# The last seven steps of a two-layer graph kernel: source order, an accumulating last gather, a second store queue

## The chip, the cores and the metric

The kernel runs on one core of one Trainium2 chip. The metric is device time in microseconds (us) of one execution. The core has a matrix engine (TensorE, PE in the profile), a vector engine (VectorE, DVE), an activation engine (ScalarE, ACT), GpSimd (POOL) and a queue engine (SyncE, SP). Each has its own instruction stream; they meet through semaphores. SP, ACT and POOL issue DMAs.

## The reference, cut to what matters

Two layers over a graph of N = 3327 nodes with 512 features and a dense 3327 x 3327 adjacency, all in float32:

```python
# layer 0: attention with the adjacency as bias
h = jnp.maximum(_layernorm(x, axis=-1), 0.0)
a = q @ k.T * scale + adj + adj                 # q, k, v: h times Wq, Wk, Wv
x = x + jax.nn.softmax(a, axis=-1) @ v
# layer 1: normalized adjacency, applied twice
h = jnp.maximum(_layernorm(x, axis=-1), 0.0)
A2 = adj + jnp.eye(N)
dscale = jnp.diagonal(A2) ** (-0.5)
temp = A2 @ h @ W.T
x = x + jax.nn.relu((dscale[:, None] * A2 * dscale[None, :]) @ temp)
```

## The kernel before

N is padded to 3328 = 26 tiles of 128 rows. After the scores, three large products remain: attention weights times h (g = 0), A2 times h (g = 1) and A2 times the scaled temp (g = 2). Each is done by a fast matrix product on two levels. On the outer level both operands are cut in halves, and seven products `p5, p1, p6, p7, p2, p3, p4` (in this order) of sums of quarters give the four quarters of the result. Each outer product has 13 x 13 tiles and is computed in two column strips, s = 0 (7 tiles wide per half) and s = 1 (6 wide). Within a strip the inner level does the same again: six pairs of tiles, t = 0 to 5, each of seven matmuls (L762) into seven PSUM banks also called p1 to p7, and a last, odd tile (t = None) with four plain matmuls (L754) into p2, p3, p4 and an eighth bank, p8 (bank 3). A matmul shows as two records in the profile.

So there are 3 x 7 x 2 x 7 steps, and `run(k)` (L963) does for step k, in this order: loads the left operand of step k+3 (`left`, L669, on SP; if the tile meets the diagonal, a 128x128 VectorE add of the identity, L686, comes with it); the matmuls; on an odd step, the gather; on VectorE the sums of step k+2 (L171 to L173, which make four sums of the loaded quarters in one of three `o` slots); what the gather left for later; and what is attached to the step in `between`. Loads go round five `a` slots.

The gather (L765) turns the eight banks into the product's four quarters: ScalarE copies p1 (L796), and VectorE does eight adds from PSUM (L797 to L806). The function `settle` then adds the product into the outer result in SBUF, whose quarters are r11 to r22; p4 goes into r21, two adds of full width (L792). For p4 of strip 1 that is split by columns into `lo` and `hi`: `settle(lo)` stands between the sixth and the seventh bank add, `settle(hi)` behind the next sums.

When rows of a result are ready, a job on them is attached to a step. For g = 0 and 1 it is a product with weights (L838, bank 3) and what follows; for g = 2 it is `finish` (L876): PE transposes the columns of a tile (L884) into a bank `pt`, ScalarE applies relu and the scale (L886), VectorE adds the loaded row `xr` (L887), and GpSimd stores it (`store`, L87). While steps still run, `pt` is bank 3; its load, `finish_load` (L871), is issued on ACT one step earlier, into a ring of four. Tiles 17, 7 and 18, 8 and 9 and 19, 10, 11 and 12, and 13 belong to steps 0 to 5 of the last strip. Of tiles 20 to 25 the right half of the features is finished earlier (in p2 to p4); the left half (256 columns) waits for the last gather and uses the six other banks.

The order of instructions on each engine is fixed in two ways. Inside the context `in_order` (L120) every engine keeps the source's order. Outside it the framework's scheduler orders each engine's instructions by its own estimate. Before, the first part ends at the last product's second strip (`last`, L982): its seven steps and the final finishes are the scheduler's.

At the very end `tc.If` (L1365) branches on a flag `bad`, computed early in group 0, to a general kernel that isn't needed here. `values_load` reads the flag into a register of each engine.

Of the kernel before, what the change touches and what calls it, by code (L numbers as in the profile page):

```python
# [15 lines left out]
P = 128  # L16
# [28 lines left out]
def graph_layers_kernel(  # L45
# [28 lines left out]
    nc = tc.nc  # L74
    N = out.shape[0]
    NP, D = x.shape
    DC = D // P
    NT = NP // P
    scale = 1.0 / math.sqrt(D)
    E = D // 2  # L80

    def pieces(n):

        m = n - n % 16
        return [(0, m), (m, n)] if m and m < n else [(0, n)]

    def store(dst, src, n):  # L87
        for a, z in pieces(n):
            nc.gpsimd.dma_start(dst[a:z], src[a:z])  # L89

# [15 lines left out]
    def bank(k, name):  # L106
        return banks.tile([P, BW], F32, name=name, tag=f"bank{k}")

    def ring(*slots):

        turn = itertools.cycle(slots)

        def take(shape, name):
            kind, k = next(turn)
            return kind(k, shape, name)

        return take
# [47 lines left out]
    x1d = [dram.tile([P, D], F32, name=f"x1d{i}") for i in range(NT)]  # L165
# [62 lines left out]
    class Chain:  # L228
# [60 lines left out]
    ps = [bank(k, "mm") for k in range(DC)]  # L289
# [116 lines left out]
    class Pair:  # L406
# [97 lines left out]
    steps = [(n, t) for n in range(len(groups)) for t in range(HALF)]  # L504
# [32 lines left out]
    with in_order(*(e.engine for e in (nc.vector, nc.tensor, nc.gpsimd, nc.sync))):  # L537
# [9 lines left out]
        k = len(steps)  # L547
# [18 lines left out]
    def seven():  # L566
        return {r: bank(ROLE[r], r) for r in ("p1", "p6", "p7", "p5", "p2", "p3", "p4")}
# [82 lines left out]
    cts = {}  # L650

    def set_up():

        free = [view(k, j)[:, 2 * m : 2 * m + 2] for k, j in ((2, 2), (3, 0), (3, 1), (3, 2)) for m in range(2)]
        free = [f.rearrange("p a w -> p (a w)") for f in free] + [mid(k, [P, H[0]], f"ct{k}") for k in range(10)]
        for s in range(2):
            cts[s] = [[free.pop()[:, : H[s]] for d in range(DC)] for y in range(2)]
        cts["to"] = [free.pop() for k in range(2)]
# [4 lines left out]
    ts_ring = ring(*spare[:3])  # L663
    xr_ring = ring(*spare[:3], (half, 14))
    out_ring = ring((half, 12), (half, 13), *spare[3:])
    xr_last = ring(*((half, k) for k in (4, 5, 6, 7)), (mid, 10), (mid, 11))
    out_last = ring((half, 12), (half, 13), *spare[2:], (half, 14))

    def left(g, s, what, t):  # L669
# [19 lines left out]
    class Right:  # L689
# [9 lines left out]
        def rows(self, dst, h, z):  # L699

            for k, i in enumerate(self.its):
                src = rowd[self.g][h * HALF + i]
                nc.sync.dma_start(dst[:, k], src if z is None else src[:, z * E : (z + 1) * E])
# [58 lines left out]
                nc.tensor.matmul(ps[r][:, :w], b[:, i], m, start=self.t == 0,  # L762
                                 stop=self.t == PAIRS - 1 and r in ("p1", "p5", "p6", "p7"))

    def gather(ct, r, s, ps):  # L765

        hw, qw = H[s], Q[s]

        def region(y, z):
            return [ct[y][2 * z + k] for k in range(2)]  # L770

        place = {"p5": (1, 1), "p1": (0, 0)}.get(r)
        if place:
            to = region(*place)
        else:
            to = [cts["to"][k][:, :hw] for k in range(2)]
        p = {k: v[:, :qw] for k, v in ps.items()}
        lo, hi = slice(0, qw), slice(qw, hw)
        r11, r12, r21, r22 = region(0, 0), region(0, 1), region(1, 0), region(1, 1)

        def settle(w):

            for k in range(2):
                if r == "p6":
                    nc.vector.tensor_sub(r12[k][:, w], to[k][:, w], r11[k][:, w])
                elif r == "p7":
                    nc.vector.tensor_add(r21[k][:, w], to[k][:, w], r12[k][:, w])  # L787
                    nc.vector.tensor_sub(r12[k][:, w], r22[k][:, w], r12[k][:, w])  # L788
                    nc.vector.tensor_sub(r22[k][:, w], r21[k][:, w], r22[k][:, w])  # L789
                elif not place:  # L790
                    into = {"p2": r11, "p3": r12, "p4": r21}[r]
                    nc.vector.tensor_add(into[k][:, w], into[k][:, w], to[k][:, w])  # L792


        c11, c12, c21, c22 = to[0][:, lo], to[1][:, lo], to[0][:, hi], to[1][:, hi]
        nc.scalar.copy(c11, p["p1"])  # L796
        nc.vector.tensor_sub(c22, p["p6"], c11)  # L797
        nc.vector.tensor_add(c21, c22, p["p7"])
        nc.vector.tensor_sub(c12, c22, p["p5"])
        nc.vector.tensor_sub(c22, c21, p["p5"])  # L800
        nc.vector.tensor_add(c11, c11, p["p2"])
        nc.vector.tensor_sub(c12, p["p3"], c12)
        if r == "p4" and s == 1:
            settle(lo)
        nc.vector.tensor_add(c21, c21, p["p4"])
        nc.vector.tensor_add(c22, c22, p["p8"])  # L806
        return lambda: settle(hi if r == "p4" and s == 1 else slice(0, hw))

    def where(i):

        s = int(i >= STRIPS[1])
        return (s, *divmod(i - STRIPS[s], HT[s]))
# [55 lines left out]

    xrs = {}

    def finish_load(i, z=(0, 1), spot=None):  # L871
        c0, c1 = z[0] * E, (z[-1] + 1) * E
        xrs[i] = (xr_ring if spot is None else xr_last)([P, D], "xr")
        nc.scalar.dma_start(xrs[i][:, c0:c1], x1d[i][:, c0:c1])

    def finish(i, z=(0, 1), spot=None):  # L876

        s, y, k = where(i)
        n = min(P, N - i * P)
        c0, c1 = z[0] * E, (z[-1] + 1) * E  # L880
        xr = xrs[i]
        pt = bank(ROLE["p8"] if spot is None else spot, "pt")
        for d in range(c0 // P, c1 // P):
            nc.tensor.transpose(pt[:, d * P : (d + 1) * P], cts[s][y][d][:, k * P : (k + 1) * P], ident)  # L884
        o = (out_ring if spot is None else out_last)([P, D], "r")
        nc.scalar.activation(o[:, c0:c1], pt[:, c0:c1], AF.Relu, scale=sd[:, i : i + 1])  # L886
        nc.vector.tensor_add(o[:, c0:c1], o[:, c0:c1], xr[:, c0:c1])  # L887
        store(out[i * P : i * P + n, c0:c1], o[:n, c0:c1], n)

    every = (*range(PAIRS), None)  # L890
    rights = {(g, r, t): Right(g, r, t) for g in range(3) for r in ORDER for t in every}
    steps = [Step(g, r, s, t, rights[g, r, t]) for g in range(3) for r in ORDER for s in range(2) for t in every]
# [3 lines left out]
    def number_of(g, r, s, t):  # L896
        return ((g * len(ORDER) + r) * 2 + s) * len(every) + t
# [5 lines left out]
    for g in range(3):  # L903
        for n, r in enumerate(ORDER):
            for t, e in enumerate(every):
                k = number_of(g, n, 0, t)
# [11 lines left out]
    for n, job in enumerate(jobs):  # L918
        k = k0 + n * (k1 - k0) // len(jobs)
# [3 lines left out]
    def rows(g, k, i, *z):  # L923

        if g == 0:
            at(k - 1, attend_load, i)
            at(k, attend, i)
            at(k + 1, attended, i)
        elif g == 1:
            at(k, temp, i)  # L930
        else:
            at(k - 1, finish_load, i, *z)
            at(k, finish, i, *z)
# [12 lines left out]
                rows(g, number_of(g + 1, 0, 0, 0) + 2 * k, i)  # L946
    for t, i in enumerate((17, 18, 19)):
        rows(2, number_of(2, 6, 1, t), i)
    for t, i in enumerate(range(20, NT)):
        rows(2, number_of(2, 4, 0, t), i, (1,))  # L950
    for k, what in ((1, totals), (2, prepare), (6, prepared), (8, judge), (9, judged)):
# [9 lines left out]
    banks_of = {}  # L961

    def run(k):  # L963
        step = steps[k]
        if k + 3 < len(steps):
            steps[k + 3].load()
        if step.t == 0:
            banks_of.update(seven())
        if not cts:
            set_up()  # L970
        if step.t is None:
            banks_of["p8"] = bank(ROLE["p8"], "p8")
        step.multiply(banks_of)
        rest = gather(cts[step.s], step.r, step.s, banks_of) if step.t is None else None
        if k + 2 < len(steps):
            steps[k + 2].sums()
        if rest:
            rest()
        for what, args in between.get(k, ()):
            what(*args)  # L980

    last = number_of(2, 6, 1, 0)  # L982
    with in_order(*(e.engine for e in (nc.vector, nc.tensor, nc.gpsimd, nc.scalar, nc.sync))):
        for k in range(last):
            run(k)
    for k in range(last, len(steps)):
        run(k)
    for i in range(20, NT):
        finish_load(i, (0,), True)
    for n, i in enumerate(range(20, NT)):  # L990
        finish(i, (0,), (0, 2, 4, 6, 7, 1)[n])


@with_exitstack
def general_kernel(
# [373 lines left out]
```

## Time and profile before

| | |
|---|---|
| median of 4 runs | 2242.48 us (2237.17 to 2244.7) |
| the profiled execution | 2238.98 us |
| its span, first to last instruction | 2236.8 us |
| granted TensorE clock, mean | 0.994 |
| PE busy | 2181.8 us |
| VectorE busy | 1623.4 us |
| ScalarE busy | 230.8 us |
| last L887 add, end | 2222.63 us |
| last store of GpSimd, start | 2224.4 us |
| matmuls of L754 of the last step, start | 2215.28 us |

Times within the profile count from the start of the span. A line of the timeline is: start, length, engine, source line, operation, tiles written and read, shape, count of like instructions merged, and in brackets how long the engine had been idle before it and what ended that. In the chain of waits each line is: start, length, what the end was waiting for in that stretch. A stretch of merged instructions lasts from the first's start to the last's end, and records of one engine overlap by some hundredths of a microsecond, so what an instruction costs is read from the distance between starts.

### The profile page before, as it was taken

What the parts mean: (1) busy time and instruction counts of PE and PEld (TensorE: products, weight loads), DVE (VectorE), ACT (ScalarE), POOL (GpSimd) and SP (SyncE); (2) the same over time, 40 slices, a digit from 0 to 9 for tenths busy, and PEclk for the clock granted to TensorE, in tenths of its full rate; (3) what the DMA queues carried; (4) which work ended last, traced back from release to release, by engine and by line L of the source; (5) the groups of instructions that cost most, each with busy time, mean ns of one, the idle gap of its engine ahead of it and who ended that gap; (6) DMA issues with size and microseconds to landing.
All of it is one profiled execution on the core that took longest, in us unless ns stands there. A gap on an engine that the chain in (4) does not pass through costs nothing. (4 is left out here: it accounts for less than half of the span.)

```text
span 2236.8 us, 20973 instructions
## 1 busy us (share of the span) xinstructions
PE 2181.8 (98%) x6252; PEld 1162.9 (52%) x6252; DVE 1623.4 (73%) x3095; ACT 230.8 (10%) x336; POOL 357.0 (16%) x555
## 2 busy tenths in 40 slices
PE   8999999999999999999999999999999999999996
PEld 4555555455555555555444555555554555555554
DVE  6369888788877788877777778886543458777775
ACT  4422121112110000000010000000000000000011
POOL 4223333333321000001222110000000000000001
PEclk9999999999999999999999999999999999999998
DMA  6668888888969898887787899876636458765684
GB/s 242 209 209 302 295 296 285 303 283 308 356 203 334 322 367 282 281 300 270 259 297 241 300 340 344 288 276 201 220 120 202 145 170 296 243 200 185 210 302 153
DMA packets 246412, 583.68 MB, mean 261 GB/s; under 512 B 34770, under 2 KB 105904, under 8 KB 246288
## 3 DMA queue, kind: packets, MB, share of 16 engines
q1 hardware_dynamic: 191968, 399.15, 53.9%
q0 software_dynamic: 45104, 167.88, 19.8%
q10 hardware_dynamic: 9216, 15.21, 2.2%
q8 instruction: 52, 0.85, 0.2%
q14 instruction: 72, 0.59, 0.1%
HBM read 414.28 MB, written 167.85 MB: 260 GB/s over the span
## 5 line engine op out<-in xcount | busy, mean ns | idle before, releaser
L762 PE MATMUL p<-part,b 128*128 128x448 f32 (+1 forms) x3528 | 1256.2, 514 | 6.9 <-DVE part L172 4.9
L762 PEld LDWEIGHTS p<-part,b 128*128 128x128 f32 x3528 | 668.2, 190 | 575.2 <-issue 301.0
L171 DVE TENSOR_TENSOR part<-part 128x896 f32<-128x896 f32 (+1 forms) x252 | 256.9, 1019 | 85.8 <-PE p L762 38.4
L439 PE MATMUL Y<-qt,hp 128*128 128x448 f32 (+1 forms) x832 | 308.9, 514 | 4.2 <-DVE g L443 3.1
L439 PEld LDWEIGHTS Y<-qt,hp 128*128 128x128 f32 x832 | 157.2, 190 | 139.8 <-issue 73.0
L439 PE MATMUL Z<-qt,hp 128*128 128x384 f32 (+1 forms) x416 | 162.6, 513 | 0.0
L173 DVE TENSOR_TENSOR part<-part,part 128x448 f32<-128x448 f32 (+1 forms) x219 | 129.5, 591 | 17.5 <-PE p L762 0.9
L172 DVE TENSOR_TENSOR part<-part,part 128x448 f32<-128x448 f32 (+1 forms) x219 | 129.4, 591 | 7.3
L838 PE MATMUL p<-w,ct 128*128 128x512 f32 x272 | 125.5, 601 | 5.3 <-DVE part L850 3.6
L754 PE MATMUL p<-part,b 128*128 128x448 f32 (+1 forms) x336 | 124.2, 513 | 0.0
L439 PEld LDWEIGHTS Z<-qt,hp 128*128 128x128 f32 x416 | 78.8, 190 | 67.4 <-issue 36.2
L443 DVE SCALAR_TENSOR_TENSOR g<-g,Y 128x384 f32<-128x384 f32 (+1 forms) x156 | 91.4, 586 | 27.1 <-PE Y L439 24.6
L832 POOL DMA_DIRECT2D sum<-job x52 | 28.4, 547 | 488.2 <-DVE job L829 269.1
L797 DVE TENSOR_TENSOR part<-p,part 128x384 f32<-128x384 f32 (+1 forms) x33 | 19.3, 586 | 104.3 <-ACT part L796 57.1
L754 PEld LDWEIGHTS p<-part,b 128*128 128x128 f32 x336 | 63.5, 190 | 53.7 <-issue 32.6
L838 PEld LDWEIGHTS p<-w,ct 128*128 128x128 f32 x272 | 51.8, 192 | 67.3 <-issue 52.0
L796 ACT COPY part<-p 128x384 f32<-128x384 f32 (+1 forms) x33 | 16.5, 499 | 669.1 <-PE p L762 669.1
L439 PE MATMUL X<-qt,hp 128*128 128x384 f32 (+1 forms) x208 | 81.1, 512 | 0.0
L446 ACT ACTIVATE g<-g 128x768 f32<-128x768 f32 (+1 forms) x48 | 43.0, 896 | 352.4 <-DVE g L443 296.5
L838 PE MATMUL p<-w,part 128*128 128x512 f32 x144 | 67.6, 607 | 5.2 <-DVE ct L806 5.2
L431 POOL DMA_DIRECT2D sum<-o x52 | 36.8, 708 | 220.1 <-DVE o L425 155.6
L89 POOL DMA_DIRECT2D out_dram<-r x34 | 18.4, 542 | 305.0 <-DVE r L887 276.5
(157 smaller groups left out, 1868.8 us busy)
## 6 DMA issues: line engine op xcount, KB each, us to landing
part<-sum SPq DMA_DIRECT2D x104, 448.0 KB, 5.2
part<-p SPq DMA_DIRECT2D x91, 448.0 KB, 6.3
part<-sum SPq DMA_DIRECT2D x104, 384.0 KB, 3.5
part<-p SPq DMA_DIRECT2D x91, 384.0 KB, 4.2
part<-in_adjT_dram SPq DMA_DIRECT2D x78, 448.0 KB, 4.9
b<-row SPq DMA_DIRECT2D x234, 128.0 KB, 4.9
part<-in_adjT_dram SPq DMA_DIRECT2D x78, 384.0 KB, 3.7
g<-in_adjT_dram SPq DMA_DIRECT2D x52, 448.0 KB, 4.5
```

Source lines behind the costliest of these rows:

```text
L171: nc.vector.tensor_add(o[:, 0:2], g[:, 0:4:3], g[:, 1:2].to_broadcast([P, 2, g.shape[-1]]))
L172: nc.vector.tensor_add(o[:, 2], o[:, 1], g[:, 0])
L173: nc.vector.tensor_add(o[:, 3], o[:, 2], g[:, 2])
L431: nc.gpsimd.dma_start(self.to(sumd)[:, 0:2], self.o)
L439: nc.tensor.matmul(ps[:, :wd], h_of(self.t, name, k), qt[B[name]][:, k], start=start and k == 0, stop=k == 1, skip_group_check=True)
L443: nc.vector.scalar_tensor_tensor(a[n], a[n], 2.0, ps[:, :wd], op0=ALU.mult, op1=ALU.add if sign > 0 else ALU.subtract)
L446: nc.scalar.activation(g[1], g[1], AF.Exp, **({"bias": pad} if self.t == HALF - 1 else {}))
L754: nc.tensor.matmul(ps[("p2", "p3", "p4", "p8")[k]][:, :w], b[:, z], a[:, 0, y], start=k == 3, stop=True)
L762: nc.tensor.matmul(ps[r][:, :w], b[:, i], m, start=self.t == 0, stop=self.t == PAIRS - 1 and r in ("p1", "p5", "p6", "p7"))
L797: nc.vector.tensor_sub(c22, p["p6"], c11)
L832: nc.gpsimd.dma_start(sumd[self.s][self.j][:, 2 + self.k], self.a)
L838: nc.tensor.matmul(ps, cts[s][y][d][:, k * P : (k + 1) * P], w[d], start=d == 0, stop=d == DC - 1)
```

## The change

Four edits. First, the last gather of all (p4, strip 1, g = 2) adds straight into r21: the first four bank adds are made into a scratch tile as before, four adds bring them into the four pieces of r21, and four more add the banks p2, p3, p4 and p8 directly. In the two earlier groups the gather of p4, strip 1, is now like all others: eight bank adds, the sums, and then one settle of full width. Second, `in_order` now spans all steps and the final finishes; the loads of the left halves of tiles 20 to 25 are attached to steps 2, 3 and 4 of the last strip, two at a time, into three tiles. Third, the last finishes store by GpSimd and SP in turn (the tile of 127 rows, number 25, has two pieces, both on SP). Fourth, the flag is read within the last gather, after the four adds into r21, on every engine.

```diff
-    def store(dst, src, n):
+    def store(dst, src, n, queue=nc.gpsimd):
         for a, z in pieces(n):
-            nc.gpsimd.dma_start(dst[a:z], src[a:z])
+            queue.dma_start(dst[a:z], src[a:z])
...
-    xr_last = ring(*((half, k) for k in (4, 5, 6, 7)), (mid, 10), (mid, 11))
+    xr_last = ring(*((half, k) for k in (4, 5, 6)))
...
-        def settle(w):
-
-            for k in range(2):
-                if r == "p6":
-                    nc.vector.tensor_sub(r12[k][:, w], to[k][:, w], r11[k][:, w])
...
+        into = r21 if last else None
...
-        nc.vector.tensor_add(c11, c11, p["p2"])
-        nc.vector.tensor_sub(c12, p["p3"], c12)
-        if r == "p4" and s == 1:
-            settle(lo)
-        nc.vector.tensor_add(c21, c21, p["p4"])
-        nc.vector.tensor_add(c22, c22, p["p8"])
-        return lambda: settle(hi if r == "p4" and s == 1 else slice(0, hw))
+        if into is None:
+            nc.vector.tensor_add(c11, c11, p["p2"])
+            nc.vector.tensor_sub(c12, p["p3"], c12)
+            nc.vector.tensor_add(c21, c21, p["p4"])
+            nc.vector.tensor_add(c22, c22, p["p8"])
+        else:
+
+            o11, o12, o21, o22 = (t[k][:, w] for t, k, w in ((into, 0, lo), (into, 1, lo), (into, 0, hi), (into, 1, hi)))
+            nc.vector.tensor_add(o11, o11, c11)
+            nc.vector.tensor_sub(o12, o12, c12)
+            nc.vector.tensor_add(o21, o21, c21)
+            nc.vector.tensor_add(o22, o22, c22)
+            flags.append(nc.values_load(bad, min_val=0, max_val=1))
+            for o, k in ((o11, "p2"), (o12, "p3"), (o21, "p4"), (o22, "p8")):
+                nc.vector.tensor_add(o, o, p[k])
+
+        def settle():
+            for k in range(2):
...
+                elif not place and into is None:
+                    t = {"p2": r11, "p3": r12, "p4": r21}[r]
+                    nc.vector.tensor_add(t[k], t[k], to[k])
...
+    def last_load(i):
+
+        xr = xr_last([P, 2, E], "xr")
+        for k in range(2):
+            xrs[i + k] = xr[:, k]
+            nc.scalar.dma_start(xr[:, k], x1d[i + k][:, 0:E])
...
+    for n, i in enumerate(range(20, NT, 2)):
+        at(number_of(2, 6, 1, 2) + n, last_load, i)
...
-    last = number_of(2, 6, 1, 0)
     with in_order(*(e.engine for e in (nc.vector, nc.tensor, nc.gpsimd, nc.scalar, nc.sync))):
-        for k in range(last):
+        for k in range(len(steps)):
             run(k)
-    for k in range(last, len(steps)):
-        run(k)
-    for i in range(20, NT):
-        finish_load(i, (0,), True)
-    for n, i in enumerate(range(20, NT)):
-        finish(i, (0,), (0, 2, 4, 6, 7, 1)[n])
-
+        for n, i in enumerate(range(20, NT)):
+            finish(i, (0,), (0, 2, 4, 6, 7, 1)[n], (nc.gpsimd, nc.sync)[n % 2])
+    return flags[0]
...
-            graph_layers_kernel(tc, x_in, *rest, out, bad)
-            with tc.If(nc.values_load(bad, min_val=0, max_val=1) > 0):
+            with tc.If(graph_layers_kernel(tc, x_in, *rest, out, bad) > 0):
                 general_kernel(tc, x_in[: x.shape[0]], adj_in, *rest, out)
```

More of the change, by code (lines that the diff above doesn't have):

```diff
@@ L763, in multiply, with gather @@
                                  stop=self.t == PAIRS - 1 and r in ("p1", "p5", "p6", "p7"))
-    def gather(ct, r, s, ps):
+    flags = []
+    def gather(ct, r, s, ps, last):
         hw, qw = H[s], Q[s]
@@ L779, in gather @@
         r11, r12, r21, r22 = region(0, 0), region(0, 1), region(1, 0), region(1, 1)
-        def settle(w):
-            for k in range(2):
-                if r == "p6":
-                    nc.vector.tensor_sub(r12[k][:, w], to[k][:, w], r11[k][:, w])
[L786 to L792, printed above, removed]
+        into = r21 if last else None
         c11, c12, c21, c22 = to[0][:, lo], to[1][:, lo], to[0][:, hi], to[1][:, hi]
@@ L800, in gather @@
         nc.vector.tensor_sub(c22, c21, p["p5"])
-        nc.vector.tensor_add(c11, c11, p["p2"])
-        nc.vector.tensor_sub(c12, p["p3"], c12)
-        if r == "p4" and s == 1:
-            settle(lo)
-        nc.vector.tensor_add(c21, c21, p["p4"])
-        nc.vector.tensor_add(c22, c22, p["p8"])
-        return lambda: settle(hi if r == "p4" and s == 1 else slice(0, hw))
+        if into is None:
[14 more added lines that the diff above has]
+            for k in range(2):
+                if r == "p6":
+                    nc.vector.tensor_sub(r12[k], to[k], r11[k])
+                elif r == "p7":
+                    nc.vector.tensor_add(r21[k], to[k], r12[k])
+                    nc.vector.tensor_sub(r12[k], r22[k], r12[k])
+                    nc.vector.tensor_sub(r22[k], r21[k], r22[k])
+                elif not place and into is None:
+                    t = {"p2": r11, "p3": r12, "p4": r21}[r]
+                    nc.vector.tensor_add(t[k], t[k], to[k])
+        return settle
     def where(i):
@@ L869, in graph_layers_kernel, with finish_load, finish @@
     xrs = {}
-    def finish_load(i, z=(0, 1), spot=None):
+    def finish_load(i, z=(0, 1)):
         c0, c1 = z[0] * E, (z[-1] + 1) * E
-        xrs[i] = (xr_ring if spot is None else xr_last)([P, D], "xr")
+        xrs[i] = xr_ring([P, D], "xr")
         nc.scalar.dma_start(xrs[i][:, c0:c1], x1d[i][:, c0:c1])
-    def finish(i, z=(0, 1), spot=None):
+    def last_load(i):
[3 more added lines that the diff above has]
+            nc.scalar.dma_start(xr[:, k], x1d[i + k][:, 0:E])
+    def finish(i, z=(0, 1), spot=None, queue=nc.gpsimd):
         s, y, k = where(i)
@@ L887, in finish @@
         nc.vector.tensor_add(o[:, c0:c1], o[:, c0:c1], xr[:, c0:c1])
-        store(out[i * P : i * P + n, c0:c1], o[:n, c0:c1], n)
+        store(out[i * P : i * P + n, c0:c1], o[:n, c0:c1], n, queue)
     every = (*range(PAIRS), None)
@@ L973, in run @@
         step.multiply(banks_of)
-        rest = gather(cts[step.s], step.r, step.s, banks_of) if step.t is None else None
+        rest = gather(cts[step.s], step.r, step.s, banks_of, k == len(steps) - 1) if step.t is None else None
         if k + 2 < len(steps):
```

## The prediction

> **What bounds the kernel now.** I read the page first, then the chain of waits from 2150 us on, then the timeline of the places that the diff touches, then each line's view of the instructions after the last store.
>
> ```profile
> PE 2181.8 (98%) x6252; PEld 1162.9 (52%) x6252; DVE 1623.4 (73%) x3095; ACT 230.8 (10%) x336; POOL 357.0 (16%) x555
> ```
> TensorE is busy for 98% of the span: any idle put into PE's order counts in full unless a later wait takes it up. In the last seven steps (from 2182.5 us) the chain of waits is PE with one break, then stores:
>
> ```profile
> 2179.30 5.14 DMA part<-in_adjT_dram
> 2184.44 0.02 issue
> 2184.46 0.29 DVE part L686
> 2184.76 0.54 DVE part L800
> 2185.30 0.04 issue
> 2185.34 2.85 PE p L762 x8
> ...
> 2211.78 0.66 PE p L762 x2
> ...
> 2223.31 1.09 POOL out_dram L89 x2
> ```
> VectorE, in the middle of the gather of p4, strip 0, took up the diagonal add L686 of a later tile, waited for its load, and PE waited 0.69 us for the bank that L800 reads. The timeline shows the rest:
>
> ```profile
> 2200.39 0.60 PE L884 MATMUL pt<-ident,ct 128*128 128x128 f32 x4
> ...
> 2200.83 1.46 PE L762 MATMUL p<-part,b 128*128 128x384 f32 x4
> ...
> 2201.17 0.69 ACT L886 ACTIVATE r<-pt,sd 128x512 f32<-128x512 f32 x1 [1.19 <-PE pt L884]
> ...
> 2202.12 0.38 PE L884 MATMUL pt<-ident,ct 128*128 128x128 f32 x2
> ...
> 2211.45 0.56 DVE L797 TENSOR_TENSOR part<-p,part 128x384 f32<-128x384 f32 x1
> ...
> 2214.84 0.60 PE L884 MATMUL pt<-ident,ct 128*128 128x128 f32 x4
> ...
> 2220.47 2.16 DVE L887 TENSOR_TENSOR r<-r,xr 128x256 f32<-128x256 f32 x6
> ...
> 2221.18 3.73 POOL L89 DMA_DIRECT2D out_dram<-r  x7 [3.06 <-DVE r L887]
> ```
> Every pt of a finish in a step is the same PSUM bank, so its transposes wait until ScalarE has read the one before. Here matmuls of the next step (two, four PE records) lie between two finishes, and PE never idles. At 2211.45 the last gather begins, before the last full step ends at 2214.84 (call this time T, the transposes of tile 13). After the stores GpSimd still has this to do (two lines' views: instruction, count, shortest, median and longest ns, first and last start):
>
> ```profile
> L1365 POOLq EVENT_SEMAPHORE  x5: 17/43/43, 2228.1 to 2228.5; - x5
> ...
> L1365 POOLq TENSOR_LOAD <-bad x1: 486/486/486, 2224.2 to 2224.2; - x1
> ...
> L1365 POOLq INC_SWDGE_SEM  x1: 1596/1596/1596, 2228.6 to 2228.6; - x1
> ...
> L1360 POOLq DRAIN  x3: 40/107/5786, 2230.2 to 2236.5; - x3
> ```
> The reader is to see that the flag's load ends at about 2224.7 and the next thing is at 2228.1, when the last store (begun 2224.40, landing 2.6 to 4.2 us after) is in. The load has 3.4 us of cover.
>
> [...] where two L838 groups follow each other on this bank with ScalarE between (1698.94, 1703.36), PE idles 0.83 us. [...] I take PE costs from distances between starts (four transposes 0.44 us in the chain, not 0.60), and one op that waits holds all behind it, as L686 did. [...] Trace: 0.54 us for a store on GpSimd, 0.33 for an issue on SP or ACT.
>
> **The change part by part.**
>
> 1. Source order in the last steps: PE. Order by step is now: step 1, finishes 7 and 18; step 2, finishes 8, 9 and 19; step 3, 10; step 4, 11 and 12; step 5, 13. Nothing lies between the finishes of one step, so four of them (18, 9, 19, 12) wait for ScalarE. From the rows: ScalarE starts 0.64 us after the transposes do (2209.45 to 2210.09, and five more), takes 0.69, and PE goes on 0.26 later (2201.86 to 2202.12): 1.59 us, of which 0.44 is the transposes. Stall 1.15 each. Bounds: 1.0, by the L838 pair (4.42 between starts less 3.43 of work), and 1.44, if ScalarE starts 0.93 late as at 2203.05, where a load was issued first. I take 1.15: in the new ACT order no load stands between Act 8 and 9 or 11 and 12. **+4.6 us** (4.0 to 5.8). PE is the bound there, so nothing hides it.
>
> 2. Source order: VectorE. L686 of step 3 now comes after the gather and its settle. The gather's eight adds run from about 2181.3 at 0.53 to 0.73 us, so the p5 bank is free at 2183.8, before PE wants it at 2184.5: **-0.7 us**. What is late next: the sums of step 1 now follow the gather, L172 done at about 2187.5, wanted at 2188.2. Later sums have some 6 us. Queued behind the finishes' adds are only the next sums, wanted a step (4.5 us) later or more.
>
> 3. Source order: loads. SP's loads keep their order; each still waits for the slot of five loads before. The small loads for tiles 20 to 25 move from the start of the stage to steps 2 to 4 on ACT, and are wanted 10 us later. [...] Cost nothing; if wrong, one load of 5.1 us against 6 us of slack.
>
> 4. The gather's end. Before, L797 to L800 ran under the last step's matmuls. Now VectorE's order puts add 13 ahead of them, and ScalarE's puts Act 13 ahead of the copy: Act 13 T+0.64 to 1.33, add 13 to about T+2.0, copy done T+1.76. First gather add T+2.0; four adds by the old starts (0.67, 0.47, 0.58, 0.47) to T+4.19; four outer adds at 0.47 to T+6.06; VectorE's flag load (550 ns in its row) costs the part that the add before it doesn't cover, about 0.2; four adds of the banks from T+6.25 to T+8.2. The two-pass adds that go (four of 0.47) are paid by the four outer adds: no count is saved, and the outer adds end three microseconds after the last matmuls, so they aren't ahead of them in time. Transposes of tiles 20 to 22 want the second bank add (T+7.3), those of 23 to 25 the fourth. ScalarE T+7.7, then 0.40 to 0.42 each, ends T+10.1; add 24 ends at T+10.14, add 25 at T+10.5. Before, the last add ended at T+7.79.
>
> 5. Two queues. GpSimd had seven stores behind one another, the last begun at T+9.56, 1.8 us behind the last add. Now its third and last is tile 24's, 0.29 us behind its add: T+10.43. **+0.9 us**. SP's four (tile 25's two at T+10.8 and 11.1) land at about T+14.5 by the loads' 3.1 us, inside the 8 us that GpSimd's INC_SWDGE_SEM and DRAIN still take. Bounds: 0 if the flag load costs nothing and the stores land faster with fewer behind them, +2.5 if VectorE empties for the flag load and SP's stores decide.
>
> 6. The flag's load: out of the tail on GpSimd, where 3.4 us covered it: nothing. On PE and ACT it falls into their wait for the adds. On SP it leaves 697 us for the end: nothing.
>
> 7. What the diff does not say: the gathers of p4, strip 1, of the two earlier groups lose their split settle.
>
> ```profile
> 1719.30 1.02 DVE L792 TENSOR_TENSOR part<-part,part 128x384 f32<-128x384 f32 x2
> ...
> 1722.69 3.60 PE L838 MATMUL p<-w,part 128*128 128x512 f32 x8
> ...
> 1723.49 1.02 DVE L792 TENSOR_TENSOR part<-part,part 128x384 f32<-128x384 f32 x2
> ```
> The first half of tile 20's columns was settled at 1720.3; now it comes after two bank adds and the sums: 1722.55 to 1724.45 for the pair of whole settles (0.95 each). PE wants the first at 1722.85 (chain) and gets it at 1723.6, the second likewise: **+0.85 us**; later PE waits hang on PE's own ends, so it stays. At the earlier boundary the same costs 1.9 us at 1171.5, but PE idles 4.52 us at 1216.41 behind a chain of ACT loads and VectorE that doesn't hang on PE: nothing.
>
> Sum: 4.6 - 0.7 + 0.9 + 0.85 = **+5.65 us**. Against the profiled execution (span 2236.8, time 2238.98) that is 2244.6; the median of the four runs is 3.5 us above that one, so the forecast is 2242.48 + 5.65 = 2248.1 us, +0.25%. What this kernel's measurement can tell from no change is 0.3%, 6.7 us.
>
> **Rivals.**
> - Slower by over 0.3%: ScalarE becomes what the last steps wait for. If its order (Act, loads that wait for a slot, Act) delays the read to the 0.93 us seen at 2203.05, four stalls cost 1.44, 5.8 in all, and with the tail's +2.5: 5.8 - 0.7 + 2.5 + 0.85 = +8.5, 2251. It decides from 1.42 us a stall, the tail being as forecast (or from +2.0 in the tail at 1.15). For it: at 2203.05 it happened; against: there the load stood in between, and now mostly doesn't.
> - No loss or a gain: the end hangs on what GpSimd still has in flight. If its 5.79 us DRAIN waits for software stores and three in place of seven shorten it by half, -2.9: +2.8, 2245; if it all but goes, -5.7: 2242.5. For it: it is the longest piece behind the last store; against: it begins 2 us after the stores are in. To be faster by 0.3% the stalls would have to go unseen as well: 2236.
> - The change doesn't do what it says: the orders and queues it does bring, instruction by instruction; the overlap of the outer adds with the last matmuls it doesn't (step 4), and that is in the sum.
>
> **How the numbers follow.** Forecast, +3.5 to +7.5: 0.60, about a quarter of it above 6.7. Slower rival, +7.5 to +13: 0.27. Rival of the shorter end: 0.13, a third of it faster. So slower 0.15 + 0.27 = 0.42, faster 0.04, same 0.54. Range 2243.5 (DRAIN halved, medians off by 1.5) to 2254.5.
>
> **What would show it.** PE waits of about 1 us for ACT before the second transposes of a step, four in all; none at the gather of p4, strip 0; a new wait of about 0.8 us at the second boundary's first weights matmul; the first gather add about 2 us behind tile 13's transposes; DRAIN at 5.8 us. Wrong if transposes follow each other without idle, if GpSimd's pieces after the last store shrink, or if the last store starts earlier than T+9.6.

## The result

The changed kernel takes 2244.56 us at the median (42 runs, 2237.62 to 2252.26), the one before 2238.95 us beside it (63 runs). The ratio on record is 1.0021, with a 95% interval of 1.0015 to 1.0027: +4.7 us, between 3.4 and 6.0 (the two medians alone would give 1.0025). That is a loss, and a smaller one than 0.3%, as forecast (+5.65 us, "same" the likeliest). In microseconds the forecast, 2248.1, is 3.5 too high: the four runs of the kernel before that it was built on had a median 3.5 us above that of the 63. The result lies only 1.1 us above the lower end of the range. The profiled execution took 2242.95 us, its span is 2241.1 us, 4.3 more than before.

### The profile page after: what moved, and what is told of

Its sections match the earlier page's. It is cut to its first block, busy times and chain, and to the rows that moved or that the text cites. A ratio compares the mean times of both kernels' runs of the same rounds, so it can differ in the third digit from the quotient of the medians.

```text
span 2241.1 us, 20975 instructions
## 1 busy us (share of the span) xinstructions
PE 2186.5 (98%) x6252; PEld 1166.2 (52%) x6252; DVE 1624.7 (72%) x3091; ACT 230.9 (10%) x336; POOL 354.9 (16%) x551
## 3 DMA queue, kind: packets, MB, share of 16 engines
q0 software_dynamic: 44928, 167.49, 19.7%
## 5 line engine op out<-in xcount | busy, mean ns | idle before, releaser
L762 PE MATMUL p<-part,b 128*128 128x448 f32 (+1 forms) x3528 | 1254.5, 514 | 5.2 <-DVE part L172 4.9
L762 PEld LDWEIGHTS p<-part,b 128*128 128x128 f32 x3528 | 668.7, 190 | 573.3 <-issue 302.8
L172 DVE TENSOR_TENSOR part<-part,part 128x448 f32<-128x448 f32 (+1 forms) x219 | 129.5, 591 | 7.4
L862 DVE SCALAR_TENSOR_TENSOR part<-p,rs,part 128x512 f32<-128x512 f32 x26 | 19.5, 750 | 66.2 <-PE p L850 57.7
```

The costliest lines, as they stand in the source:

```text
L172: nc.vector.tensor_add(o[:, 2], o[:, 1], g[:, 0])
L862: nc.vector.scalar_tensor_tensor(xt, ps, rs[:, i : i + 1], xt, op0=ALU.mult, op1=ALU.add)
```

## The profile after

The page's line of busy time, for the changed kernel:

```profile
PE 2186.5 (98%) x6252; PEld 1166.2 (52%) x6252; DVE 1624.7 (72%) x3091; ACT 230.9 (10%) x336; POOL 354.9 (16%) x551
```

No matmul was added, and still PE's busy time is 4.7 us longer: the mean granted clock is 0.991 here and was 0.994, and busy time contains that (14 records of L762 from 2017.85 us on took 8.20 us, most of it at a granted clock of 0.50, and the next 14, at 1.00, took 5.43). Stalls have to be read elsewhere. The chain of waits in the last strip (start, length, what was waited for):

```profile
2194.04 0.45 PE pt L903 x4
2194.49 0.02 issue
2194.51 0.70 ACT r L905
2195.21 0.04 issue
2195.25 0.66 PE pt L903 x4
2195.91 4.52 PE p L762 x14
2200.43 0.45 PE pt L903 x4
...
2203.73 4.52 PE p L762 x14
```

Before, ScalarE (ACT) wasn't in this part of the chain at all. Here the second finish's transposes start only 0.04 us after ScalarE has read the bank. From the first transposes to the next matmuls it is 1.87 us (2194.04 to 2195.91) for two finishes that need 0.88 of work: 0.99 us lost. With three finishes in the step it is 3.30 for 1.32 (2200.43 to 2203.73): 1.98. The timeline of the same kernel shows all places that the prediction named:

```profile
1723.69 3.71 PE L850 MATMUL p<-w,part 128*128 128x512 f32 x8 [0.70 <-DVE part L817]
...
2184.40 4.68 PE L762 MATMUL p<-part,b 128*128 128x384 f32 x14
...
2195.25 0.44 PE L903 MATMUL pt<-ident,ct 128*128 128x128 f32 x2 [0.78 <-ACT r L905]
...
2201.64 0.66 PE L903 MATMUL pt<-ident,ct 128*128 128x128 f32 x4 [0.78 <-ACT r L905]
2203.07 0.44 PE L903 MATMUL pt<-ident,ct 128*128 128x128 f32 x2 [0.78 <-ACT r L905]
...
2214.42 0.66 PE L903 MATMUL pt<-ident,ct 128*128 128x128 f32 x4 [0.78 <-ACT r L905]
...
2219.43 0.60 PE L903 MATMUL pt<-ident,ct 128*128 128x128 f32 x4
...
2221.39 0.55 DVE L787 TENSOR_TENSOR part<-p,part 128x384 f32<-128x384 f32 x1
...
2223.57 0.55 DVE L799 TENSOR_TENSOR part<-part,part 128x384 f32<-128x384 f32 x1
...
2225.45 1.94 DVE L805 TENSOR_TENSOR part<-part,p 128x384 f32<-128x384 f32 x4
...
2229.96 0.55 POOL L89 DMA_DIRECT2D out_dram<-r  x1 [0.31 <-DVE r L906]
```

From top to bottom: the wait of 0.70 us at the second boundary; the first step of the last strip in one piece of 14 records, with no wait for L790 in its middle; four stalls behind ScalarE; tile 13's transposes at T = 2219.43; the gather from T+1.96, its adds into r21 (L799) from T+4.1, well behind the last matmuls; the bank adds from T+6.02; GpSimd's last store at T+10.53. What GpSimd does after that, by the two lines' views (count, shortest/median/longest ns, first to last start):

```profile
L1380 POOLq EVENT_SEMAPHORE  x5: 17/43/115, 2230.4 to 2233.1; - x5
...
L1380 POOLq INC_SWDGE_SEM  x1: 1516/1516/1516, 2233.2 to 2233.2; - x1
...
L1376 POOLq DRAIN  x3: 40/107/5459, 2234.8 to 2240.8; - x3
```

DRAIN took 5459 ns where it took 5786, INC_SWDGE_SEM 1516 where it took 1596, and they began 3.3 us after the last store's start, before 4.2. So the span ends 21.7 us after T, before 22.0, though the last store starts 1.0 us later. A store by GpSimd is called a software store below: the page gives q0 (167.49 MB, GpSimd's) as software_dynamic, and q1 and q10 (SP's and ACT's: from 2200 us on they moved 0.39 MB, SP's four stores, and 1.84 MB, ACT's loads) as hardware_dynamic.

The stage from the strip's first L762 to T shows a part that the prediction missed. The timeline before:

```profile
2188.46 4.97 PE L762 MATMUL p<-part,b 128*128 128x384 f32 x14
...
2188.48 0.29 DVE L686 TENSOR_TENSOR part<-part,ident 128x128 f32<-128x128 f32 x1 [0.20 <-DMA part<-in_adjT_dram]
2188.69 0.55 DVE L172 TENSOR_TENSOR part<-part,part 128x384 f32<-128x384 f32 x1
```

14 records of this step take 4.68 us elsewhere; here a second diagonal add waited for its load ahead of the sums that PE wanted, and the step took 4.97. In all the stage lasted 32.29 us before and 35.03 after, and 31.05 in a kernel that has source order without the stalls (below). So source order took 1.24 us away against this profile, and the stalls put 3.98 on top.

## The experiments

All ratios are to the kernel before, over runs on the same chip, with 95% intervals. In every run I read two lengths in the trace: the stage (first L762 of the last strip to T) and the tail (T to the end of the span). With 0.97 us for the boundary where the settle is of full width (PE was 0.14 us late just ahead of it in the changed kernel, and 1.12 late at 1764.30) they give a sum against before. The spans are given to 0.1 us, so the tails are good to 0.05. All thirteen sums lie within the measured intervals:

| kernel | stage | tail | sum, us | measured, us |
|---|---|---|---|---|
| before | 32.29 | 21.96 | | |
| changed | 35.03 | 21.67 | +3.4 | +4.7 (3.4 to 6.0) |
| x1 split settle | 35.03 | 21.29 | +2.1 | +1.8 (0 to 3.4) |
| x2 finishes apart | 31.05 | 21.32 | -0.9 | +0.7 (-2.5 to 3.6) |
| x3 one queue | 35.03 | 23.83 | +5.6 | +5.6 (3.8 to 7.4) |
| x4 order only | 35.02 | 23.97 | +4.7 | +3.4 (1.6 to 5.2) |
| x5 queues only | 32.67 | 19.43 | -2.2 | -2.5 (-4.0 to -1.1) |
| x6 flag at end | 35.02 | 22.32 | +4.1 | +4.5 (2.2 to 6.9) |
| x7 gather ahead | 35.02 | 20.64 | +2.4 | +2.5 (0.9 to 4.3) |
| x8 all | 31.04 | 20.44 | -2.8 | -4.0 (-5.8 to -2.2) |
| x9 SP alone | 35.02 | 18.57 | +0.3 | +2.0 (0.2 to 4.0) |
| x10 all, no software stores | 31.04 | 14.83 | -8.4 | -7.8 (-10.3 to -5.1) |
| x11 before, no software stores | 32.02 | 14.53 | -7.7 | -9.4 (-12.3 to -6.5) |
| x12 settle only | 32.57 | 22.20 | +1.5 | +1.3 (-0.7 to 3.4) |

That is a coarse test, as the intervals reach 1.3 to 3.1 us each way, and the misses have a pattern. Measured less sum is +0.7 us on average in the seven kernels whose settle is of full width (changed, x2, x3, x6, x7, x9, x12), and -0.7 in the six with the split one. So the sum seems to lack a cost of the full-width settle; point 7 below finds one at the first boundary.

In source order the stage is the same in every trace, 35.02 us or, without the stalls, 31.04. In the scheduler's order (before, x5, x11, x12) it goes from 32.0 to 32.7, as PE's waits in it, for VectorE behind the two diagonal adds, add up to 0.4 to 1.1 us. A difference of half a microsecond between two of these four says nothing of the edit.

**x2: the stalls.** In the last strip, the second and third finish of a step wait and are written between two matmuls of the next step.

```diff
+                if held and r in ("p6", "p5"):
+                    finish(*held.pop(0))
...
+            if what == finish and number_of(2, 6, 1, 0) <= k:
+                done += 1
+                if done > 1:
+                    held.append(args)
+                    continue
```

> The changed kernel with the second and third finish of a step of the last strip put between matmuls of the next step (behind p6 and p5), so that no two finishes follow each other on the one bank; the rest stays as changed. Theory (four stalls of PE for ScalarE's read, about 1.0 us each by the changed kernel's profile): all four go, the last strip is 4.0 us shorter, ratio to before 1.0003. Rival (the last strip is longer by order on VectorE or by loads, and PE's stalls only take up a wait that would come anyway): PE waits elsewhere instead, ratio 1.0015 or more.

Ratio 1.0003 (0.9989 to 1.0016), the theory's number; the interval just reaches the rival's 1.0015, so it is the trace that decides. The timeline:

```profile
2191.40 0.60 PE L905 MATMUL pt<-ident,ct 128*128 128x128 f32 x4
2191.84 1.46 PE L762 MATMUL p<-part,b 128*128 128x384 f32 x4
2193.13 0.38 PE L905 MATMUL pt<-ident,ct 128*128 128x128 f32 x2
```

Two matmuls (1.29 us from start to start) stand between two finishes, and no transpose waits any more. The stage is 3.98 us shorter, as the theory had it. That the stalls cost this much of PE's time, with nothing taking their place, is shown.

**x4: source order alone**, on the kernel before (gather, settle, stores and flag as they were). The diff shows the order alone; the loads of tiles 20 to 25 move to steps 2 to 4 as well.

```diff
-        for k in range(last):
+        for k in range(len(steps)):
             run(k)
-    for k in range(last, len(steps)):
-        run(k)
-    for i in range(20, NT):
-        finish_load(i, (0,), True)
-    for n, i in enumerate(range(20, NT)):
-        finish(i, (0,), (0, 2, 4, 6, 7, 1)[n])
+        for n, i in enumerate(range(20, NT)):
+            finish(i, (0,), (0, 2, 4, 6, 7, 1)[n])
```

> The kernel before with source order over all steps and the final finishes, and with the loads of the left halves at steps 2 to 4; gather, settle, stores by GpSimd and flag at the end stay as before. Theory (order is what costs): +4.0 us by the four stalls, -0.7 at the gather of p4, strip 0, and a last gather that begins 2 us after tile 13's transposes in place of 3.4 us ahead of them, with seven stores on one queue: +2.4 us at the last store; together +5.7, ratio 1.0025. Rival (the new gather, the flag and the settle are what costs, and the order is harmless): ratio 1.0005 or less.

Ratio 1.0015 (1.0007 to 1.0023): less than the theory's 1.0025, more than the rival's 1.0005. The stage has the same 35.02 us as the changed kernel's, so all of it is the order. The tail grew by 2.0 us. Source order alone makes the kernel slower. The trace's sum is +4.7 where the theory had +5.7: 0.5 of that is the stage's -1.24 in place of -0.7, 0.4 the tail.

**x1 and x12: the settle**, from both sides: x1 puts the split back into the changed kernel (the diff shows the place of the first half), x12 takes it out of the one before.

```diff
             nc.vector.tensor_sub(c12, p["p3"], c12)
+            if r == "p4" and s == 1:
+                settle(lo)
             nc.vector.tensor_add(c21, c21, p["p4"])
```

> The changed kernel with the split settle of p4, strip 1, put back for the two earlier groups (settle(lo) between the sixth and seventh bank add); the rest stays as changed. Theory (the lost split costs PE 0.85 us at the second boundary, and that stays): the weights matmul at about 1723.5 is reached without a wait for VectorE, and the time is 0.9 us below the changed kernel's, ratio to before 1.0017 where the changed kernel has 1.0021. Rival (the wait is made up for later, because VectorE and the loads set the pace again before the end): the wait at 1723.7 goes all the same, but the last strip begins no earlier and the ratio stays at 1.0021.

> The kernel before with the split settle taken away for the two earlier groups and nothing else. Theory (0.85 us at the second boundary, nothing at the first): PE waits 0.7 us for VectorE at the boundary near 1723, ratio 1.0004. Rival (it costs what the ratio of the run with the split put back would have, about 2.9 us): 1.0013. Third (the wait is made up for before the end): 1.0000, with the wait all the same.

x1: 1.0008 (1.0000 to 1.0015); x12: 1.0006 (0.9997 to 1.0015). In x1's timeline the weights matmul follows with no wait (first line); in x12's it has one (second line), in a kernel that differs from the one before by nothing else:

```profile
1726.65 3.60 PE L852 MATMUL p<-w,part 128*128 128x512 f32 x8
...
1727.66 3.71 PE L839 MATMUL p<-w,part 128*128 128x512 f32 x8 [0.70 <-DVE part L792]
```

So the wait belongs to the full-width settle. The price of that settle isn't fixed by the times. In x1 both expectations missed: 1.0017 and 1.0021 lie above its interval, and it came out 2.9 us below the changed kernel where 0.9 was expected. In x12 all three lie within. The trace has 0.97 at this boundary, and there is a second place where the settle costs (point 7 below).

**x3: all last stores on GpSimd** again, the rest as changed.

```diff
-            finish(i, (0,), (0, 2, 4, 6, 7, 1)[n], (nc.gpsimd, nc.sync)[n % 2])
+            finish(i, (0,), (0, 2, 4, 6, 7, 1)[n], nc.gpsimd)
```

> The changed kernel with all seven last stores on GpSimd; the rest stays as changed. Theory (a queue costs its issue time alone): seven stores at 0.54 us behind one another put the last one's start 1.5 us later, what comes after the last store stays at 11.1 us, ratio 1.0028. Rival (the end after the last store grows with the number of software stores: 12.4 us with seven before, 11.1 with three after): 2.8 us later, ratio 1.0034. Third (SP's stores held the end): no difference, 1.0021 or less.

Ratio 1.0025 (1.0017 to 1.0033). The theory's 1.0028 and the third's 1.0021 lie within, the rival's 1.0034 just outside, too near to part them. The trace does in part. GpSimd's timeline:

```profile
2226.59 3.75 POOL L89 DMA_DIRECT2D out_dram<-r  x7 [5.94 <-DVE r L906]
```

The seventh of them starts 0.53 before the end of the row, at T+12.0: 1.5 us later than in the changed kernel, the theory's number. The view of the line of DRAIN:

```profile
L1376 POOLq DRAIN  x3: 40/107/5786, 2234.9 to 2241.3; - x3
```

It is back at 5786 ns. Of the rival's further 1.3 us, 0.6 is there, and 0.4 of that is DRAIN and INC_SWDGE_SEM.

**x5: two queues alone**, on the kernel before.

```diff
-        finish(i, (0,), (0, 2, 4, 6, 7, 1)[n])
+        finish(i, (0,), (0, 2, 4, 6, 7, 1)[n], (nc.gpsimd, nc.sync)[n % 2])
```

> The kernel before with nothing changed but the queues of the last stores (GpSimd and SP in turn). Theory (GpSimd's end shrinks with the number of its software stores, 12.4 us after the last store's start with ten of them in flight or just done, 11.1 in the changed kernel): last store of GpSimd 1.4 us earlier, the rest 1.2 us shorter, -2.6 us, ratio 0.9988. Rival (a queue costs its issue time alone): -1.4 us, 0.9994. Third (SP's stores now end last): 1.000 or more.

Ratio 0.9989 (0.9982 to 0.9995): this part of the change alone gains 2.5 us (the theory's number; the rival's 0.9994 lies within the interval too). The last store starts at 2222.19, T+7.7, in place of T+9.6, and what comes after it takes 11.8 us in place of 12.4, so the trace has both parts of the theory, the first larger and the second smaller than expected. The two lines' views:

```profile
L1365 POOLq INC_SWDGE_SEM  x1: 1516/1516/1516, 2226.1 to 2226.1; - x1
...
L1360 POOLq DRAIN  x3: 40/107/5459, 2227.7 to 2233.7; - x3
```

In the changed kernel this gain pays for a gather that ends later.

**x6: the flag read at the end**, by every engine ahead of the branch, with the rest as changed.

```diff
-            flags.append(nc.values_load(bad, min_val=0, max_val=1))
...
-            with tc.If(graph_layers_kernel(tc, x_in, *rest, out, bad) > 0):
+            graph_layers_kernel(tc, x_in, *rest, out, bad)
+            with tc.If(nc.values_load(bad, min_val=0, max_val=1) > 0):
```

> The changed kernel with the flag read where it was before, by every engine ahead of the branch, in place of in the last gather. Theory (the read costs nothing in either place: in the gather it lies under the adds, at the end under GpSimd's wait for its last store): ratio 1.0021 as the changed kernel, last store to end as there, 11.1 us. Rival (the read at the end delays GpSimd's end by its 0.5 to 0.8 us, or the one in the gather delays VectorE): ratio off by 0.0002 to 0.0004, which the time can't show, but the profile can.

Ratio 1.0020 (1.0010 to 1.0031). The bank adds start at T+6.02 with the flag's load between them and the adds ahead, and at T+6.02 without: on VectorE it costs nothing. At the end GpSimd's load lies between 2233.2 and 2234.0, and its wait lasts until 2237.5, so it hides there too. The last store to the end took 12.1 us against the 11.1 expected; that is the wait for the stores (4.3 us from the last one's start against 3.3), which is as long in x7 and x8, where the flag is read in the gather (4.4 and 4.6).

**x7: the first half of the last gather one step earlier**, ahead of finish 13.

```diff
+        if k == len(steps) - 2:
+            gather(cts[step.s], step.r, step.s, banks_of, True, 0)
         if k + 2 < len(steps):
             steps[k + 2].sums()
```

> The changed kernel with the first half of the last gather (copy of p1, four bank adds, four adds into r21) written one step earlier, right behind the last full step's matmuls and ahead of finish 13; its other half (flag, four bank adds) stays. Theory (in the changed kernel the outer adds don't run ahead of the last matmuls but 4.2 to 6.0 us behind tile 13's transposes, and put off everything after them): last bank add at T+4.1 in place of T+8.1, last store of GpSimd at T+6.4 in place of T+10.5, time 4.1 us below the changed kernel's, ratio 1.0003. Rival (GpSimd's and SP's end doesn't hang on the last store): the adds come earlier, ratio unchanged at 1.0021.

Ratio 1.0011 (1.0004 to 1.0019): half of the gain expected. The timeline shows what held it:

```profile
2216.17 1.98 ACTq L896 DMA_DIRECT2D xr<-x1d  x2
2218.19 0.48 ACT L787 COPY part<-p 128x384 f32<-128x384 f32 x1 [1.76 <-PE p L762]
...
2220.89 0.55 DVE L801 TENSOR_TENSOR part<-part,part 128x384 f32<-128x384 f32 x1
...
2223.37 1.94 DVE L808 TENSOR_TENSOR part<-part,p 128x384 f32<-128x384 f32 x4
```

The brackets name PE, but p1's bank had long been done (T = 2220.06, and the copy starts at T-1.9): ScalarE's queue was held by two loads, 1.98 us, and the copy starts the moment they end. From there VectorE runs without a gap through nine adds, and the bank adds start at T+3.3, the last store at T+8.4 rather than T+6.4. I had counted VectorE's adds from T-3.

**x8: x1, x2 and x7 together.**

> The changed kernel with three edits together: split settle kept for the two earlier groups, finishes put apart, first half of the last gather written a step earlier. Theory (the costs add up): stalls +0, gather of p4, strip 0, -0.7, boundary 0, tail from T to the end 17.5 us in place of 22.0 before: together -5.2 us against before, ratio 0.9977. Rival (one of them is made up for by a wait elsewhere): 0.999 or more.

Ratio 0.9982 (0.9974 to 0.9990), faster than both kernels. The theory's 0.9977 lies within, but not for the reason given: its tail was to be 17.5 us and is 20.4. Stage 31.04; the copy is on time here (T-2.4), yet VectorE begins at T-1.7, needs 4.1 us for its eight adds, and has finish 13's add ahead of the bank adds. These start at T+3.0 and the last add ends at T+8.1, no earlier than before (T+7.8). What the tail gains has to come from the two queues, which alone gained more (x5).

**x9: all last stores on SP**, the rest as changed (`nc.sync` for all in x3's line).

> The changed kernel with all seven last stores on SP, so that GpSimd's last store is tile 13's, at about T+2.7. Theory (what holds the end is GpSimd's wait for its last software store and its drain, 11.1 us behind that store's start): GpSimd is done by T+14, and SP's last store (T+11.5 to 13 by its seven issues of 0.35 to 1.2 us) with a landing of 2.3 to 4.0 us sets the end at T+16 to T+18 in place of 21.7; -4 us against the changed kernel, ratio 1.0003. Rival (the end is a fixed 10 us of the program behind whatever is last): the end at T+22 to 24, ratio 1.0025.

Ratio 1.0009 (1.0001 to 1.0018), which holds the theory's 1.0003 and not the rival's 1.0025. The tail is 18.6 us, 3.1 shorter, though all seven are issued by one engine, and 0.6 longer than the theory's upper end. SP issues from 2232.54 to 2237.33; the two lines' views of SP and GpSimd:

```profile
L1380 SPq EVENT_SEMAPHORE  x8: 17/17/17, 2240.1 to 2240.6; - x8
...
L1380 POOLq INC_SWDGE_SEM  x1: 1456/1456/1456, 2228.9 to 2228.9; - x1
...
L1376 POOLq DRAIN  x3: 40/170/5214, 2230.4 to 2242.4; - x3
```

GpSimd's long DRAIN now lies beside the work: it is over at 2235.6, and SP's stores set the end, 5.4 us behind the last issue.

**x10 and x11: no last store on GpSimd.** Tiles 20 to 24 on SP, tile 25's two on ACT, whose own work is over by then; x10 on top of x8, x11 on the kernel before with nothing else changed.

```diff
-        finish(i, (0,), (0, 2, 4, 6, 7, 1)[n])
+        finish(i, (0,), (0, 2, 4, 6, 7, 1)[n], (nc.sync, nc.sync, nc.sync, nc.sync, nc.sync, nc.scalar)[n])
```

> The kernel with split settle kept, finishes apart and the last gather's first half a step earlier, with the last stores of tiles 20 to 24 on SP and tile 25's two on ACT, so that none is on GpSimd. Theory (GpSimd's wait and drain behind its last software store set the end; without them the end is 5.4 us behind the last issue, as with all seven on SP): last issue at about T+9, end at T+14.5 in place of T+20.4 with every second store on GpSimd; ratio 0.9955. Rival (seven issues of up to 1.2 us on SP and ACT make up for it): end at T+18 or later, ratio 0.997 or more.

> The kernel before with nothing changed but the queues of the last stores: tiles 20 to 24 on SP, tile 25's two pieces on ACT. Theory (as above; the order of the last steps, the old gather and the flag at the end are kept): end at T+14 to 15.5 in place of T+22.0, ratio 0.9969. Rival (the end isn't GpSimd's, and the gain by two queues was the shorter row of stores alone): ratio 0.9985 or more.

x10: 0.9965 (0.9954 to 0.9977, six runs); x11: 0.9958 (0.9945 to 0.9971, five runs). x11's timeline of ACT's and SP's stores:

```profile
2218.69 1.65 ACTq L89 DMA_DIRECT2D out_dram<-r  x2
...
2216.93 3.17 SPq L89 DMA_DIRECT2D out_dram<-r  x5
```

and the views of the two lines behind them, SP's wait for its stores and GpSimd's DRAIN:

```profile
L1365 SPq EVENT_SEMAPHORE  x8: 17/17/17, 2222.8 to 2223.3; - x8
...
L1360 POOLq DRAIN  x3: 40/169/5214, 2217.9 to 2225.1; - x3
```

T is 2210.87; the last issue ends at T+9.5, when GpSimd's last store began before, but the span ends at T+14.5 and not at T+22.0. GpSimd's DRAIN is over at 2223.1, and GpSimd then waits until 2224.2, so DRAIN no longer sets the end. One edit of queues takes 9.4 us off (6.5 to 12.3), and beats both kernels. x10, with everything else repaired, isn't measurably faster than that; the two intervals overlap, and its tail is no shorter (14.8). Not tried: x11 together with source order and finishes apart, which would leave out x10's gather.

## Why the prediction was right, and where not

Its sum was +5.65 us; the trace has +3.4 by the same terms, the times +4.7. That the times came this close is in part luck. By the traces the stalls were put 0.6 us too high, the gain by VectorE's order 0.5 too low and the tail 1.2 too long, while the first boundary, put at nothing, seems to have cost some 1.5 (point 7).

The two profiles' spans differ by 4.3 us. Of the 0.9 that the sum leaves, 0.1 lies ahead of the second boundary, as what is left of larger differences both ways (the changed kernel's profile was 2.6 ahead at 1165 us). 0.7 lies between 2017 and 2151 us, where the diff touches nothing. PE's idle ahead of it is the same in both traces, 0.56 and 2.53 us with one transpose between. The clock granted after it isn't: it was 0.50 for 6.8 us in the changed kernel and for 3.4 before, and the first 14 records of L762 took 8.20 us and 6.67, where the next 14 took 5.43 in both. That makes 1.5 us; 0.8 came back by 2151, where PE waited 0.79 us for VectorE (2145.78) in the profile before alone. Why the slow stretch was longer behind the same idle isn't shown. One pair of profiles is thus good for a microsecond or two, not for tenths.

1. The four stalls: right in place and number; 1.0 us each and not 1.15, the low bound, which the L838 pair had given. The 0.26 us that I added for PE's start after ScalarE (2201.86 to 2202.12) was 0.04 where PE had nothing else to do: in the row that I took it from, PE had been busy with matmuls until then.
2. VectorE's order: right in sign, -1.24 and not -0.7 (-1.0 to -1.6 by which of the four traces in the scheduler's order one takes). I took only the first interruption by L686; the second one, at 2188.48, held up L172 and PE by another 0.3, and the first cost 0.85.
3. The loads: nothing in the changed kernel, as said. In x7 they did cost: the two loads ahead of the copy held ScalarE's queue for 1.98 us. That is what a queue of loads can cost once something early is put behind it.
4. The gather's end: right. First add T+1.96 (T+2.0 forecast), bank adds T+6.02 (6.25; the flag's 0.2 wasn't there), last add ends T+10.67 (10.5).
5. The last store at T+10.53 (10.43): right. The step that failed is the one after it: "+0.9" for the tail was -0.3, as what follows the last store took 1.3 us less. Of that, 0.41 is DRAIN and INC_SWDGE_SEM, which hang on the number of software stores; I had held these at 8 us. That these pieces shrink was among the prediction's own signs of being wrong. The other 0.9 is the wait for the stores, which scatters from 3.3 to 4.6 us over runs with the same stores (3.3 in the changed kernel, 4.3 in x6), so no part of it can be put down to the change. I had counted the second queue for issue time alone, and that led me here: for the end of the program it counts which engine issued, by 7.4 us in x11.
6. The flag: nothing, shown by x6.
7. The boundaries. At the second, 0.85 was forecast and the trace has 0.97, with a wait of 0.70 shown by x12. At the first, "nothing" doesn't hold. PE's wait there is as forecast, about 1.9 us, but the idle at 1216.41 doesn't take it up. Before:

```profile
1205.60 0.75 DVE L850 SCALAR_TENSOR_TENSOR part<-p,rs,part 128x512 f32<-128x512 f32 x1 [1.78 <-DMA part<-in_x_dram]
...
1216.41 5.40 PE L838 MATMUL p<-w,part 128*128 128x512 f32 x8 [4.52 <-DVE ct L806]
```

and in the changed kernel:

```profile
1170.77 3.71 PE L850 MATMUL p<-w,part 128*128 128x512 f32 x8 [1.78 <-DVE part L817]
...
1204.45 0.75 DVE L862 SCALAR_TENSOR_TENSOR part<-p,rs,part 128x512 f32<-128x512 f32 x1 [3.58 <-DMA part<-in_x_dram]
...
1215.27 6.68 PE L850 MATMUL p<-w,part 128*128 128x512 f32 x8 [4.61 <-DVE ct L795]
```

The idle is as long as before, since the chain that ends it is later too: its load of x took 4.7 us from issue to landing, before 2.9. Over all traces it took 3.8 to 5.4 us in the seven kernels with the full-width settle and 2.8 to 3.6 in the others. Measured from 1165 us to the end of that idle, the seven lose 1.2 us on average against the profile before (from a gain of 0.6 to a loss of 2.1), and the six with the split settle gain 0.2 (from a gain of 0.7 to a loss of 0.9). About 1.5 us thus seem to be left of the wait, which fits the pattern in the table's misses and x1's 2.9 us. Why the load takes longer isn't shown.

Of the rivals, ScalarE's late reads at 0.93 us didn't happen (0.78 of idle each time). The shorter end did happen, at a seventh of the 2.9 us priced for it: DRAIN doesn't halve with fewer stores (5459 ns with three, 5786 with seven), but it can be moved off the end of the tail as a whole (in x9 it is over at 2235.6, and SP's stores end last). That rival had the right place and the wrong lever.

## What to carry to other kernels

When two jobs share a bank and another engine reads it between them, put other work between: two matmuls (1.29 us) were enough in x2, and written back to back the jobs cost about a microsecond a pair (0.99 us here) on the engine that bounds the kernel. Read the end of a program from its last software store: what GpSimd still has to do behind it (11.1 to 12.4 us in these kernels) can be longer than everything that you gain ahead of it, and storing the last tiles from SP and ACT took it off the path (a tail of 14.5 us in x11, 22.0 before). Before moving work ahead on one engine, count what is already queued there in those microseconds, loads included (1.98 us for two in x7).

## What the runs showed of the hardware

- DRAIN on GpSimd took 5786, 5459 and 5214 ns with seven, three and no last stores by GpSimd, INC_SWDGE_SEM 1596 (1592 in two runs), 1516 (1512 in two) and 1456: about 82 and 20 ns a store, on top of 6.7 us for the two that stay when none of the last stores is GpSimd's and tile 13's is its last.
- A store's record on GpSimd lasts 0.54 us, and GpSimd waited 2.5 (x10) to 4.6 us (x8) from the last one's start. In the changed kernel, from 2200 us on, GpSimd's stores landed 2.8 us (128 KB) and 3.4 us (256 KB) after their issue, at the median.
- SP's end follows its last issue by 5.4 us (x9), and there is no long DRAIN on it: 7 ns each.
